# One broadcast of B for two scans: the first product moves to the other PSUM bank pair, the second takes the broadcast's place

## The chip, the cores and the metric

The kernel runs on one core of one Trainium2 chip. A core has five engines that run side by side, each through its own queue in order: TensorE (PE in the profile, with its weight loads as PEld), VectorE (DVE), ScalarE (ACT), GpSimd (POOL) and SyncE (SP), which here issues the DMAs. The metric is the device time of one execution, in microseconds (us).

## The reference

The program is a stack of four layers on x of 32 images, 512 channels, 32 x 32 pixels, each layer x = x + f(groupnorm(x)). Layer 0 scales channels by a small network on DCT statistics, layer 1 is a grouped 3 x 3 convolution, layer 3 a channel attention. Layer 2 is the costly one: a state space model (SSM) over the pixels of each image, on three resolutions (1024, 256 and 64 positions), in both directions. Cut to what matters:

```python
def _ssm(x, xw, dtw, dtb, Al, Dv, g, be):
    xd = jnp.einsum('bdl,kd->blk', x, xw)
    dts, Bs, Cs = xd[..., :R_DT], xd[..., R_DT:R_DT + n], xd[..., R_DT + n:]
    delta = jax.nn.softplus(jnp.einsum('blr,dr->bld', dts, dtw) + dtb)
    A = -jnp.exp(Al)
    dA = jnp.exp(delta[..., None] * A)
    dBx = delta[..., None] * Bs[:, :, None, :] * xt[..., None]
    def step(h, inp):
        da, dbx, c = inp
        h = h * da + dbx
        return (h, jnp.einsum('bdn,bn->bd', h, c))
    _, ys = lax.scan(step, h0, (dA, dBx, Cs))     # over the positions
    return _layernorm(ys + xt * Dv, g, be)
```

There are 256 channels d and 16 states n. B (Bs above) depends on the state and the position alone, not on the channel.

## The kernel before, in words

Every matrix has 128 partitions. For the scans a partition is a pair of a channel and a state: 32 channels times 4 states. One scan instruction of VectorE runs over the 1024 positions of all 128 pairs at once. The 256 channels are 8 groups of 32 and the 16 states are 4 sets of 4, so one direction on the finest resolution has 8 x 4 = 32 scans; the image has two such directions (64 scans), and the two coarser resolutions together take 20 more.

`fine` (L1232) does one direction of the finest resolution. It goes over the two halves d of the channels, in each over the four sets k of states, and in each over the four channel groups q. For each (d, k, q), which is one unit of the schedule, it records these operations:

- TensorE (L1264 to L1266): a broadcast. Two matmuls with a selection matrix, `sel_b[:, k]`, copy the rows of B for the states of set k to the 32 partitions of each state, for 512 positions each. The result fills `pb`, a pair of PSUM banks. It depends on k and not on q.
- ScalarE (L1273): `da` = exp(delta x A), from `dt` in SBUF, where `dt[q]` holds delta x and delta for the channel group q, copied to the states by DMA.
- VectorE (L1279): the product `pb` = `dt` x `pb`, in place in PSUM.
- VectorE (L1212): the scan, from `da` and `pb` into `h` in SBUF.
- GpSimd (L1287): `h` = `h` x `cb`, where `cb` holds C, copied by DMA.
- TensorE (L1295), after each four units: sums over the states into the PSUM banks `y` and `y1b`. After four sets of states VectorE adds the skip term (L1309).

`both` (L1349) does the same for the coarser resolutions, with a broadcast in L1393 or L1400, the product in L1407, `da` in L1435 or L1444, and two scans, one in each direction, from the same product.

The work around the scans belongs to other images and layers: the DCT (L617), the convolution (L899), the dense products of layer 2 (`dense`, L952, called from `scan_inputs`, L989, and from the output), the convolutions that halve the resolution (`down_conv`, L974), `prepare` (L1046), which makes delta, B and C, layer norms (L1142 to L1165) and the last layer (L1670). All run between the scans of the current image.

The order is set by a planner. `Plan.op` records each operation with its engine, an assumed duration, what it reads and writes, and a key, a due time (100 per image, of which a unit of the scans takes 100 / 84). `Plan.order` then plays the recorded operations through: at every moment, each engine takes the ready operation with the smallest key, and the order that results is built as the fixed order of each engine. A `Clock` counts units; `ck.key(a)` is the due time of a units before the current one. The names of line 43 are such leads: `B_AHEAD` for the broadcast, `A_AHEAD` for `da`, `L_AHEAD` for the loads of `dt`, `DB_AHEAD` for the product. The names above it give when other work is due; `INPUTS` is the stretch over which `scan_inputs` makes f1, the input of the scans, and `DOWN` the due time of `down_conv`, which reads f1.

Buffers come from rings. The ring `pb` has two members, each a pair of PSUM banks (L288); `da` has two, `h` six. A ring may be a line (first come, first served by key): then its buffers are given out in the order of their keys, and a buffer's key is that of the first operation that touches it unless it is set by hand. An operation is not taken until the ring has a free member for it and it is that buffer's turn. A member is free once the last operation that uses it has ended.

Of the kernel before, what the change touches and what calls it, by code (L numbers as in the profile page):

```python
# [15 lines left out]
HW = 1024  # L16
# [12 lines left out]
UNITS = 84  # L29

FRONT = (30.9, 63.6)
INPUTS = (109.0, 112.0)
Z = (86.2, 90.1)
DOWN = 114.3
LOWER = (11.8, 36.0)
# [4 lines left out]
SPECTRA = (51.7, 128.4)  # L40
EVACUATE = 85.0
LN_LATE = 10.1
B_AHEAD, A_AHEAD, L_AHEAD, DB_AHEAD = 5.8, 5.9, 14.7, 1.3


class Buf:
# [192 lines left out]
def kernel(ctx: ExitStack, tc: tile.TileContext, t: dict, out: bass.AP):  # L239
    nc = tc.nc  # L240
# [155 lines left out]
    pl = Plan(rings)  # L396
# [16 lines left out]
    def pe(fn, dur, r, w, key, acq=()):  # L413
        return pl.op("PE", dur, fn, r, w, key, acq)
# [757 lines left out]
    def raised(y1, y2, key):  # L1172

        for d in range(2):
            for h in range(2):
                for a in range(2):
                    def go(d=d, h=h, a=a):
                        o = y1.t[:, d, halves[h]].rearrange("p (r a k b) -> p r a k b", a=2, k=16, b=2)
                        i = y2.t[:, d, :].rearrange("p (r k o) -> p r k o", k=16, o=1)
                        nc.gpsimd.tensor_add(  # L1180
                            o[:, :, a], o[:, :, a],
                            i[:, 8 * h : 8 * h + 8].to_broadcast([P, 8, 16, 2]),
                        )

                    pool(go, 256, [(y1, (d, h)), (y2, d)], [(y1, (d, h))], key)
# [46 lines left out]
    def fine(lv, f, pre, S, rev, ck):  # L1232


        sb, cd, dd = pre.pop(f"{lv}_{HW}")
        pl.cross = pl.BESIDE
        if rev:
            raised(S["y1"], S["y2"], ck.key())
        pl.cross = pl.CROSS
        yv = []  # L1240
        for d in range(2):
            acc = [pl.buf("y0"), pl.buf("y1b")]
            dt = []
            for q in range(4):
                ch = slice((d * 4 + q) * 32, (d * 4 + q + 1) * 32)
                z = pl.buf("dt")
                dt.append(z)
                spread(
                    lambda z=z: z.t, lambda i, ch=ch: dd.t[:, ch, :].rearrange("a c l -> c a l"),
                    P * HW * 8, [(dd, (d, h)) for h in range(2)], [z], ck.key(L_AHEAD - q),  # L1250
                )
            for k in range(NS // NQ):
                cb = pl.buf("cb")
                spread(
                    lambda cb=cb: cb.t,
                    lambda i, k=k: cd.t[k * NQ + i : k * NQ + i + 1].to_broadcast([32, HW]),
                    P * HW * 4, [cd], [cb], ck.key(5),
                )
                hs = []
                for q in range(4):  # L1260
                    g = d * 4 + q
                    pb, da, h = pl.buf("pb"), pl.buf("da"), pl.buf("h")

                    def bcast(pb=pb, k=k):  # L1264
                        for cols in halves:
                            nc.tensor.matmul(  # L1266
                                pb.t[:, cols], lhsT=sel_b[:, k, :], rhs=sb.t[:, cols],
                                start=True, stop=True,
                            )

                    pe(bcast, 0.55, [sb], [pb], ck.key(B_AHEAD))
                    act(
                        lambda da=da, z=dt[q], k=k, g=g: nc.scalar.activation(  # L1273
                            da.t, z.t[:, 1, :], AF.Exp, scale=A[lv][:, k, g : g + 1]
                        ),
                        HW, [dt[q]], [da], ck.key(A_AHEAD), True,
                    )
                    dve(
                        lambda pb=pb, z=dt[q]: nc.vector.tensor_mul(pb.t, z.t[:, 0, :], pb.t), HW,  # L1279
                        [dt[q], pb], [pb], ck.key(DB_AHEAD),  # L1280
                    )
                    pl.op(
                        "DVE", 2.21, lambda h=h, da=da, pb=pb: scan(h.t, da.t, pb.t, rev), [da, pb], [h],
                        ck.key(),
                    )
                    pool(
                        lambda h=h, cb=cb: nc.gpsimd.tensor_mul(h.t, h.t, cb.t), HW, [h, cb], [h],  # L1287
                        ck.key(),
                    )
                    hs.append(h)  # L1290
                    ck.u += 1
                for i, cols in enumerate(halves):
                    def add(i=i, cols=cols, hs=hs, acc=acc, k=k):
                        for q in range(4):
                            nc.tensor.matmul(  # L1295
                                acc[i].t[q * 32 : (q + 1) * 32, :], lhsT=sel_y, rhs=hs[q].t[:, cols],
                                start=(k == 0), stop=(k == NS // NQ - 1),
                            )

                    pe(add, 1.3, hs, [acc[i]], ck.key(2))  # L1300
            y = pl.buf("yv")
            yv.append(y)
            dma(
                lambda y=y, d=d: nc.sync.dma_start(y.t, f.t[d]), P * HW * 4, [(f, d)],
                [(y, 0), (y, 1)], ck.key(8),
            )
            for i, cols in enumerate(halves):
                dve(
                    lambda i=i, cols=cols, acc=acc, y=y, d=d: nc.vector.scalar_tensor_tensor(  # L1309
                        y.t[:, cols], in0=y.t[:, cols], scalar=Dv[lv][:, d : d + 1], in1=acc[i].t,  # L1310
                        op0=ALU.mult, op1=ALU.add,
                    ),
                    HB, [(y, i), acc[i]], [(y, i)], ck.key(3),
                )
        pl.cross = pl.BESIDE
        if not rev:
            S["y1"] = pl.buf("y1")
        y1 = S["y1"]
        for i, cols in enumerate(halves):
            yb = [(yv[d], i) for d in range(2)]  # L1320

            def yc(d, cols=cols):
                return yv[d].t[:, cols]

            def yo(d, cols=cols):
                return y1.t[:, d, cols]

            ob = [(y1, (d, i)) for d in range(2)]
            layer_norm(
                lv, yc, yb, yc if rev else yo, yb if rev else ob, HB, ck.key() + (0.0 if rev else LN_LATE)  # L1330
            )
            if not rev:
                continue
            g = pl.buf("g2")
            for d in range(2):
                dma(
                    lambda d=d, g=g, cols=cols: nc.sync.dma_start(g.t[:, d, :], S["zs"].t[d, :, cols]),
                    P * 2048, [(S["zs"], (d, i)), yb[d]], [(g, d)], ck.key(),
                )
                pool(  # L1340
                    lambda d=d, yo=yo, yc=yc: nc.gpsimd.tensor_add(yo(d), yo(d), yc(d)), HB,
                    [yb[d], ob[d]], [ob[d]], ck.key(),
                )
                pool(
                    lambda d=d, yo=yo, g=g: nc.gpsimd.tensor_mul(yo(d), yo(d), g.t[:, d, :]), HB,
                    [ob[d], (g, d)], [ob[d]], ck.key(),
                )

    def both(lv, f, pre, ysum, below, n, ck):  # L1349


        sb, cd, dd = pre.pop(f"{lv}_{n}")
# [21 lines left out]
        for d in range(2):  # L1374
            dt = pl.buf("dt")
# [9 lines left out]
                )  # L1385
            for k0 in range(0, 4, nk):
                pb = pl.buf("pb")

                def bcast(pb=pb, k0=k0):
                    for h in range(2):  # L1390
                        if nk == 1:
                            src = sb.t.rearrange("p (o l) -> p o l", o=1).to_broadcast([96, 2, n])
                            nc.tensor.matmul(  # L1393
                                pb.t[:, halves[h]].rearrange("p (o l) -> p o l", o=2),
                                lhsT=sel_b[:, k0, :], rhs=src, start=True, stop=True,
                            )
                            continue
                        for k in range(h * nk // 2, (h + 1) * nk // 2):
                            src = sb.t.rearrange("p (o l) -> p o l", o=1).to_broadcast([96, 4, n])
                            nc.tensor.matmul(  # L1400
                                pieces(pb.t)[:, k, :, :], lhsT=sel_b[:, k0 + k, :], rhs=src,
                                start=True, stop=True,
                            )
# [21 lines left out]
                for r in range(2):  # L1425
                    da, h = pl.buf("da"), pl.buf("h")
# [302 lines left out]
    def begin(b):  # L1729
# [10 lines left out]
        else:  # L1740
            p0 = 100.0 * (b - 2)
            front(b, st[b], p0 + FRONT[0], p0 + FRONT[1])
            scan_inputs(
                st[b], p0 + INPUTS[0], p0 + INPUTS[1], (p0 + Z[0], p0 + Z[1]), p0 + DOWN
            )
# [134 lines left out]
```

## Time and profile before

| | us |
|---|---|
| median of 3 runs | 11386.0 (11367.82 to 11386.98) |
| profiled execution | 11408.22 |
| its span | 11406.1 |
| TensorE busy | 9375.9 |
| VectorE busy | 9938.1 |
| ScalarE busy | 8259.6 |
| GpSimd busy | 9544.0 |
| of VectorE: 2688 scans | 6069.7 |
| of VectorE: 2048 products of `fine` | 2462.4 |
| of TensorE: 4096 broadcast matmuls of `fine` | 1390.4 |
| of GpSimd: 2048 multiplications with `cb` | 4818.1 |

The span goes from the first instruction to the last; the device time is some 2 us more. "Busy" is time in which the engine works on an instruction. A row of a group names the line, the engine, the operation, what it writes and reads, its shape and count, and after the bar its busy time in us, the mean of one in ns, and the idle time of the engine just ahead of it with what ended most of that. A row of the waits names who waited, for whom, how many us in all, how many times, and the longest. The granted clock is the share of TensorE's full clock that the chip allowed; its mean here is 0.861.

### The profile page before, as it was taken

Reading aid. Unit: us, or ns where it says so; the run is one execution under the profiler, and the core shown is the slowest. Engines: PE = TensorE matmul, PEld = TensorE weight load, DVE = VectorE, ACT = ScalarE, POOL = GpSimd, SP = SyncE. Lnnn points to the kernel's source line nnn. Section 1 sums busy time; section 2 is a strip of 40 time slices with the busy share of each in tenths; the row PEclk is TensorE's granted clock in tenths of the full one; section 3 lists DMA queues with packets and bytes.
Section 4 is the critical chain, followed back from the end, with each engine's and each line's share of the span. In section 5 each row is a group of like instructions: output and inputs, shape, how many; then the busy total and the mean of one; then the engine's idle time right before and its main releaser. Section 6 shows DMA issues by size and latency. Waiting matters only on the chain. (4 is left out here: it accounts for less than half of the span.)

```text
span 11406.1 us, 152013 instructions
## 1 busy us (share of the span) xinstructions
PE 9375.9 (82%) x47512; PEld 4155.3 (36%) x47512; DVE 9938.1 (87%) x8861; ACT 8259.6 (72%) x15684; POOL 9544.0 (84%) x7759
## 2 busy tenths in 40 slices
PE   7888888888888888888888888888888888878765
PEld 4444433334333343333333343333433333332221
DVE  1875889998899989999899999899889998999997
ACT  4677777777778777777777777777777776667664
POOL 2775878898889888888888988898888898889885
PEclk7888889888889888898888988898898987888877
DMA  5665677776767777777767777777677766776654
GB/s 153 167 173 164 182 197 195 186 194 186 212 179 202 188 188 191 204 198 202 191 183 189 204 199 189 189 189 186 190 199 196 187 180 181 199 192 185 168 134 136
DMA packets 931019, 2116.80 MB, mean 186 GB/s; under 512 B 240033, under 2 KB 372537, under 8 KB 917785
## 3 DMA queue, kind: packets, MB, share of 16 engines
q1 hardware_dynamic: 930192, 2107.01, 69.5%
q8 instruction: 376, 6.16, 0.2%
q14 instruction: 433, 3.55, 0.1%
q10 hardware_dynamic: 18, 0.09, 0.0%
HBM read 1677.04 MB, written 429.52 MB: 185 GB/s over the span
## 5 line engine op out<-in xcount | busy, mean ns | idle before, releaser
L1212 DVE TENSOR_TENSOR_SCAN h_all<-da,pb 128x1024 f32<-128x1024 f32 x2688 | 6069.7, 2275 | 296.2 <-ACT da L1435 78.3
L1287 POOL TENSOR_TENSOR h_all<-h_all,cb 128x1024 f32<-128x1024 f32 x2048 | 4818.1, 2363 | 859.9 <-DVE h_all L1212 582.7
L1273 ACT ACTIVATE da<-dt,w_Al 128x1024 f32<-128x1024 f32 x2048 | 2337.1, 1145 | 1171.5 <-DVE h_all L1212 902.5
L1279 DVE TENSOR_TENSOR pb<-dt,pb 128x1024 f32<-128x1024 f32 x2048 | 2462.4, 1218 | 322.7 <-PE pb L1266 276.1
L1266 PE MATMUL pb<-sb,sel_b 96*128 96x512 bf16 x4096 | 1390.4, 426 | 888.0 <-DVE h_all L1212 797.2
L1455 POOL TENSOR_TENSOR h_all<-h_all,cb 128x1024 f32<-128x1024 f32 x640 | 1509.3, 2363 | 20.8 <-DVE h_all L1212 7.4
L1266 PEld LDWEIGHTS <-sel_b 96*128 96x128 bf16 x4096 | 402.4, 107 | 2032.8 <-issue 1998.0
L952 PE MATMUL mm<-x,wt 128*128 128x512 f32 x2048 | 1027.8, 626 | 54.8 <-ACT x L482 18.9
L899 PE MATMUL mm<-pk,wk 99*32 99x512 f32 (+1 forms) x6024 | 904.2, 688 | 113.8 <-DMA pk<-in_xp 19.9
L1444 ACT ACTIVATE da<-dt,w_Al 128x255 f32<-128x255 f32 x2048 | 899.4, 500 | 97.6 <-DVE h_all L1212 79.7
L1295 PE MATMUL y<-h_all,w_sel_y 128*32 128x512 f32 x4096 | 784.4, 724 | 33.5 <-POOL h_all L1287 27.2
L617 PE MATMUL mm<-w_dct,sx 128*128 128x128 f32 x3968 | 651.2, 319 | 94.6 <-ACT sg L460 24.7
L617 PEld LDWEIGHTS mm<-w_dct,sx 128*128 128x128 f32 x3968 | 583.6, 225 | 237.7 <-ACT sg L460 50.1
L1295 PE MATMUL y1b<-h_all,w_sel_y 128*32 128x512 f32 x4096 | 647.7, 663 | 0.0
L952 PE MATMUL mm<-y,w_out_w 128*128 128x512 f32 x1024 | 576.2, 655 | 0.1
L952 PEld LDWEIGHTS mm<-x,wt 128*128 128x128 f32 x2048 | 387.5, 198 | 492.5 <-issue 284.5
L1112 POOL TENSOR_TENSOR g<-g,g 128x512 f32<-128x512 f32 (+2 forms) x384 | 392.9, 1023 | 144.6 <-ACT g L1111 134.5
L1096 PE MATMUL mm<-xd,dtw 64*128 64x512 f32 (+2 forms) x768 | 417.4, 628 | 79.2 <-ACT xd L1066 11.7
L1142 PE MATMUL mm<-ln,ones_d 128*128 128x512 f32 (+1 forms) x768 | 433.1, 662 | 59.9 <-ACT ln L1154 30.7
L1407 DVE TENSOR_TENSOR pb<-dt,pb 128x1024 f32<-128x1024 f32 x320 | 387.7, 1218 | 108.5 <-PE pb L1393 86.6
L974 PE MATMUL mm<-f,wt 128*128 128x256 f32 (+1 forms) x1984 | 421.6, 357 | 21.7 <-ACT f L982 6.0
L1142 PE MATMUL mm<-yv,ones_d 128*128 128x512 f32 x640 | 380.6, 691 | 40.1 <-ACT mm L921 7.2
(292 smaller groups left out, 16188.4 us busy)
## 6 DMA issues: line engine op xcount, KB each, us to landing
dt<-dd SPq DMA_DIRECT2D x2048, 256.0 KB, 7.3
cb<-cd SPq DMA_DIRECT2D x2048, 128.0 KB, 4.8
pk<-in_xp SPq DMA_DIRECT2D x753, 297.0 KB, 5.5
dd<-g SPq DMA_DIRECT2D x256, 512.0 KB, 5.1
xr<-x SPq DMA_DIRECT2D x128, 512.0 KB, 6.3
yv<-fs SPq DMA_DIRECT2D x128, 512.0 KB, 5.1
dt<-ddm SPq DMA_DIRECT2D x512, 128.0 KB, 3.9
sx<-in_x SPq DMA_DIRECT2D x124, 512.0 KB, 4.7
```

What stands on the lines that cost most here:

```text
L617: nc.tensor.matmul(ps.t[:, j * P : (j + 1) * P], lhsT=sx.t[:, 1, i : i + P], rhs=dct, start=True, stop=True,)
L899: nc.tensor.matmul(ps.t[32 * q : 32 * q + 32, r0 * IMG : r1 * IMG].rearrange("p (r k) -> p r k", k=IMG), lhsT=wk.t[:, q, 32 * dy : 32 * dy ...
L952: nc.tensor.matmul(ps.t, lhsT=w(k)[:, m * P : (m + 1) * P], rhs=r()[:, cols], start=(k == 0 and not opened), stop=(k == len(rhs) - 1),)
L1142: lambda d=d: nc.tensor.matmul(ps.t[:, 0:n], lhsT=ones_d, rhs=of(d), start=(d == 0), stop=(d == 1)),
L1212: nc.vector.tensor_tensor_scan(v[0], v[1], v[2], 0.0, ALU.mult, ALU.add)
L1266: nc.tensor.matmul(pb.t[:, cols], lhsT=sel_b[:, k, :], rhs=sb.t[:, cols], start=True, stop=True,)
L1273: lambda da=da, z=dt[q], k=k, g=g: nc.scalar.activation(da.t, z.t[:, 1, :], AF.Exp, scale=A[lv][:, k, g : g + 1]),
L1279: lambda pb=pb, z=dt[q]: nc.vector.tensor_mul(pb.t, z.t[:, 0, :], pb.t), HW,
L1287: lambda h=h, cb=cb: nc.gpsimd.tensor_mul(h.t, h.t, cb.t), HW, [h, cb], [h],
L1295: nc.tensor.matmul(acc[i].t[q * 32 : (q + 1) * 32, :], lhsT=sel_y, rhs=hs[q].t[:, cols], start=(k == 0), stop=(k == NS // NQ - 1),)
L1444: lambda da=da, quads=quads, q=q, g=g, body=body, k0=k0: nc.scalar.activation(pieces(da.t)[:, 0, q, body], quads(1)[:, q, body], AF.Exp, s ...
L1455: lambda h=h, k0=k0: nc.gpsimd.tensor_mul(pieces(h.t), pieces(h.t), cbv()[:, k0 : k0 + nk, :].rearrange("p k (o l) -> p k o l", o=1).to_br ...
```

## The change

In `fine`, two channel groups that follow each other now share one broadcast. For an even q a buffer `src` is broadcast, and a second buffer `pb` is taken from the same ring. The first product reads `src` and writes `pb`; the second product, of the odd q, reads `src` and writes `src`. The first scan reads `pb`, the second `src`. The keys of the two buffers are set by hand, 2.9 and 1.0 units ahead, since an operation that comes late would otherwise set them; the `pb` of the coarser resolutions gets a key of 2.9 units ahead too, in place of its broadcast's. Three constants are changed: the end of `INPUTS`, `B_AHEAD` and `DB_AHEAD`. In the changed kernel the lines of `fine` stand some 8 further down: the broadcast is L1273, the product L1287, the multiplication with `cb` L1295, the sums L1303, the skip term L1317, the product of `both` L1416.

```diff
-INPUTS = (109.0, 112.0)
+INPUTS = (109.0, 123.2)
...
-B_AHEAD, A_AHEAD, L_AHEAD, DB_AHEAD = 5.8, 5.9, 14.7, 1.3
+B_AHEAD, A_AHEAD, L_AHEAD, DB_AHEAD = 8.0, 5.9, 14.7, 1.8
...
-                    pb, da, h = pl.buf("pb"), pl.buf("da"), pl.buf("h")
-
-                    def bcast(pb=pb, k=k):
+                    da, h = pl.buf("da"), pl.buf("h")
+
+
+                    if q % 2 == 0:
+                        src, pb = pl.buf("pb"), pl.buf("pb")
+                        src.key, pb.key = (ck.key(2.9), len(pl.ops)), (ck.key(1.0), len(pl.ops))
+                    else:
+                        pb = src
+
+                    def bcast(pb=src, k=k):
                         for cols in halves:
...
-                    pe(bcast, 0.55, [sb], [pb], ck.key(B_AHEAD))
+                    if q % 2 == 0:
+                        pe(bcast, 0.55, [sb], [src], ck.key(B_AHEAD))
...
-                        lambda pb=pb, z=dt[q]: nc.vector.tensor_mul(pb.t, z.t[:, 0, :], pb.t), HW,
-                        [dt[q], pb], [pb], ck.key(DB_AHEAD),
+                        lambda pb=pb, src=src, z=dt[q]: nc.vector.tensor_mul(pb.t, z.t[:, 0, :], src.t), HW,
+                        [dt[q], src], [pb], ck.key(DB_AHEAD),
...
             for k0 in range(0, 4, nk):
                 pb = pl.buf("pb")
+                pb.key = (ck.key(2.9), len(pl.ops))
```

## The prediction

> **What bounds the kernel now.** First the page's busy shares and its slices: three engines stand close together.
>
> ```profile
> PE 9375.9 (82%) x47512; PEld 4155.3 (36%) x47512; DVE 9938.1 (87%) x8861; ACT 8259.6 (72%) x15684; POOL 9544.0 (84%) x7759
> ```
>
> The windows split that into stages (columns: busy time and count of each engine, then granted clock, DMA share and rate):
>
> ```profile
> 2000.00:4000.00 2000.00, 1686.23 (x8588) 732.10 (x8587) 1823.93 (x1628) 1515.08 (x2886) 1744.00 (x1412) 0.87 0.72 192
> 10000.00:11000.00 1000.00, 779.51 (x3566) 294.49 (x3566) 926.48 (x729) 693.55 (x1226) 890.61 (x679) 0.84 0.66 174
> 11000.00:11406.00 406.00, 238.84 (x727) 70.39 (x725) 328.16 (x279) 195.40 (x282) 255.60 (x159) 0.74 0.52 140
> ```
>
> In the steady part VectorE works 91% of the time, GpSimd 87%, TensorE 84%. VectorE is the fullest, so what ends its idle time sets the pace: 11406.1 - 9938.1 = 1468 us idle, about 230 us of it in the first 285 us, where it has almost nothing to do. Third, who it waits for:
>
> ```profile
> DVE pb L1279 <- PE pb L1266: 276.1, 246, 8.2
> DVE sms L663 <- POOL sms L657: 133.9, 27, 30.6
> DVE pb L1407 <- PE pb L1393: 86.6, 68, 5.1
> DVE h_all L1212 <- ACT da L1435: 78.3, 54, 6.0
> DVE yv L1309 <- PE y L1295: 70.9, 35, 6.4
> ...
> DVE sms L469 <- PE mm L466: 46.8, 23, 6.0
> DVE h_all L1212 <- PE y1b L1295: 45.6, 50, 3.4
> DVE h_all L1212 <- ACT da L1273: 39.8, 47, 4.1
> DVE pb L1279 <- DMA dt<-dd: 39.4, 38, 3.1
> ```
>
> The largest entry is the product (L1279) that waits for the broadcast (L1266), the very pair that the change touches; most of the others are results of TensorE too. Fourth, TensorE's own waits show that the two block each other:
>
> ```profile
> PE pb L1266 <- DVE h_all L1212: 797.2, 703, 5.6
> ```
>
> At 703 of the 2048 broadcasts TensorE stood still, 1.13 us each, because the bank pair to be written was still read by a scan, and everything behind it in its queue stood too. Last, the groups with the durations used below:
>
> ```profile
> L1212 DVE TENSOR_TENSOR_SCAN h_all<-da,pb 128x1024 f32<-128x1024 f32 x2688 | 6069.7, 2275 | 296.2 <-ACT da L1435 78.3
> L1273 ACT ACTIVATE da<-dt,w_Al 128x1024 f32<-128x1024 f32 x2048 | 2337.1, 1145 | 1171.5 <-DVE h_all L1212 902.5
> L1279 DVE TENSOR_TENSOR pb<-dt,pb 128x1024 f32<-128x1024 f32 x2048 | 2462.4, 1218 | 322.7 <-PE pb L1266 276.1
> L1266 PE MATMUL pb<-sb,sel_b 96*128 96x512 bf16 x4096 | 1390.4, 426 | 888.0 <-DVE h_all L1212 797.2
> L1266 PEld LDWEIGHTS <-sel_b 96*128 96x128 bf16 x4096 | 402.4, 107 | 2032.8 <-issue 1998.0
> L1407 DVE TENSOR_TENSOR pb<-dt,pb 128x1024 f32<-128x1024 f32 x320 | 387.7, 1218 | 108.5 <-PE pb L1393 86.6
> ```
>
> **What the Trainium skill says.** "Perfetto Trace Analysis", Identifying the Most-Contended Engine, takes occupancy as a fair measure for Vector and GpSimd but not for TensorE; that is why I rank VectorE first by its 87% and judge TensorE by its stops. The same page, Optimization Strategy, says that repeating gaps can mean that there is not enough SBUF or PSUM for the next tile: the 703 stops of the broadcast, each ended by a scan, agree. "VectorE: DVE Perf Modes", Why PSUM operands drop a tier, holds any fp32 operation with a PSUM operand to the plain rate, so a product that reads one bank pair and writes the other should last as long as one in place; the trace has only the in-place form (1218 ns). "TensorE: Matmul & The Clock Gate", What's actually happening, says that activity releases the throttle; the windows agree (TensorE busy 84%, clock 0.87; 78%, 0.84; 59%, 0.74), and this is a price of taking work away.
>
> **The change part by part.**
>
> *The broadcast.* Half of the 4096 matmuls of L1266 go: 1390.4 / 2 = 695 us of TensorE busy time and 201 us of weight loads. Not all of it is gained. Between the first two windows the clock falls 0.03 for 0.06 less busy share. TensorE's share goes from 0.82 to about 8681 / 11200 = 0.775, so I estimate the clock 0.024 lower, 2.8% longer matmuls, 8681 x 0.028 = 240 us back: 455 us freed. TensorE is not the fullest engine, so this counts only through VectorE's waits.
>
> *The wait of the product.* This is the main term. For every product I laid the trace's VectorE row against the built program's order, which names the bank pair of each product and scan. The cover of a broadcast is what VectorE does between the last scan of that pair and the product that needs it filled again:
>
> ```
> in between            before: products, us waited   after: first products
> nothing                    128,  76.1                      0
> one product                699, 114.7                      0
> one scan                   751,  57.3                    883
> product and scan           435,  29.7                    108
> more                        33,   0                       32
> ```
>
> A broadcast of two matmuls takes 1390.4 / 2048 = 0.68 us busy and longer with its hand-over, so a cover of one product (1.2 us) is too short and one scan (2.3 us) mostly enough. In the changed program the short covers are gone: the first scan of a pair frees the other bank pair, the broadcast runs under the second scan, and the second product of a pair needs no broadcast. At the old rates: 883 x 0.076 + 108 x 0.068 + 32 x 0.076 at most = 77 us instead of 276, that is -200 us. Bounds: -276 (no wait left) and 0 (the longer covers are eaten by TensorE's queue).
>
> *TensorE's other results.* L1407 (86.6) and the entries of L1309 on y and y1b, L469, L459 (two), L1153 and L1212 on y1b (70.9 + 26.2 + 46.8 + 30.1 + 29.2 + 31.7 + 45.6) make 367 us of VectorE waiting on TensorE. It has 455 us less to do, and with half the broadcasts at the old share and length of stops also about 400 us fewer stops. I take a quarter, -92; bounds 0 and a half, -184.
>
> *The moved product.* 1024 products write another bank pair: cost 0; were they 2% slower, 1024 x 0.024 = 25 us. They still take one PSUM input. A first product now needs both pairs, so it can no longer be put between the two scans of the pair ahead. That adds a wait only where the second of these scans is itself late, and behind it stands VectorE's whole row. Scans waited 78 + 40 + 39 = 157 us for da before; 0, with +40 as the bound if a quarter more comes of it.
>
> *Keys.* B_AHEAD 8.0 lets TensorE take the broadcast ahead of more of its other work once its pair is free; what that costs is the blocking case below. DB_AHEAD 1.8 puts both products ahead of the first scan more often; it asks for dt earlier, which cost 39.4 us before: 0, bound +40. INPUTS spreads the four f1 products over 14% of an image instead of 3%. Behind them on TensorE are the down convolutions, and behind those the coarse scans; in the built order VectorE work between the last down convolution and the first coarse product is as long as before (mostly 50 to 120 us in both), so 0, bounds -15 and +30 (L1407 waited 14.6 us for ddc). The new key on the coarse pb only sets its place among the bank pairs: in the order its broadcasts have no more cover than before, 0.
>
> *What is late next.* -200 - 92 = -292 us of VectorE idle time. A product that comes sooner meets da (ACT: 78 + 40 + 39 us in all before), dt by DMA, and GpSimd, 87% full. ACT's own idle time ahead of da is mostly waiting for scans (902 of 1171 us), so it follows VectorE rather than holds it; I give back a third, +97. Sum: -195 us.
>
> The profiled execution took 11408.2 us, 2 us more than its span, so 11213 for that one; the median of the runs shown is 22 us lower, 11386.0 - 195 = 11191. Forecast 11190.
>
> **The rivals.**
>
> *TensorE was the hidden bound.* For it: its busy and stopped time, 9376 + 797 us, rivals VectorE's 9938. Then two thirds of 276 + 86.6 + 280 = 643 us of VectorE's waits on it go, and nothing comes back: -430, 10955. Against it: GpSimd at 87% comes close behind.
>
> *The wait only moves.* The products stop waiting for broadcasts and the scans wait for da, cb's multiplication or dt instead. For it: in the order the leads of ACT, DMA and the remaining TensorE results are the same as before, and GpSimd is nearly as full. Then 0 to -60: 11355. Against it: ACT waits for scans 902 us, so it has room.
>
> *The broadcast blocks TensorE (slower).* Both bank pairs now serve one pair of scans, so each of the 1024 broadcasts is tied to the first scan of the pair ahead, and TensorE, taking it first, stands until that scan ends. If each stands a whole scan, 1024 x 2.3 = 2355 us instead of 797, less the 455 freed: +1103 us of TensorE. Before, 276 us of product waits came with 797 us of stops, 0.35 to one; so +386 - 200 = +186: 11570. It decides from 797 + 455 + 200 / 0.35 = 1823 us of stops, 1.8 us a broadcast. Against it: a broadcast stopped 0.39 us on the mean, and a stop while VectorE is busy harms only what is queued behind.
>
> That the change does not do what it says is excluded: the built program has 2048 matmuls of this kind and 2048 products.
>
> **How the numbers follow.** Forecast 0.50 (its own range 11090 to 11300), hidden bound 0.18, moved wait 0.14, blocking 0.18. A change under 0.2% (23 us) can't be told from none here. Faster by more: 0.50 + 0.18 + 0.07 = 0.75, less 0.01 for the forecast's tail = 0.74; same 0.05 (from the moved wait); slower 0.18 + 0.03 = 0.21. The range reaches from 10930, just past the hidden bound, to 11420, the moved wait with the keys' +40; most of the blocking case is left out.
>
> **What would show it.** Right: the wait of the first product (L1287 then) for its broadcast under 120 us; VectorE 88 to 90% busy with unchanged busy time; TensorE busy near 8900 with a clock near 0.84; its stops at the broadcast near 400 us. Wrong: those stops above 1800 us, waits of scans for da or of L1309 for y grown by more than 200 us together, or a product clearly above 1218 ns.

## The result, and the profile after

The changed kernel takes 11295.67 us (median of 4 runs, 11285.95 to 11315.67); the kernel before, run beside it, takes 11384.6 us. The ratio is 0.9924, with a 95% interval of 0.9912 to 0.9936: faster by 0.76%, or 89 us, where 195 us were forecast. The profiled execution took 11294.69 us, 113.5 us less than that of before; the latter lay some 22 us above its median.

The busy shares on the page of the changed kernel:

```profile
PE 9004.9 (80%) x45464; PEld 3951.5 (35%) x45464; DVE 9955.1 (88%) x8861; ACT 8260.1 (73%) x15684; POOL 9544.7 (85%) x7759
```

TensorE lost 371 us of busy time. Who VectorE waits for (who, for whom, us in all, times, longest):

```profile
DVE sms L663 <- POOL sms L657: 146.4, 28, 29.4
DVE pb L1287 <- PE pb L1273: 116.0, 104, 5.9
DVE pb L1287 <- DMA dt<-dd: 89.9, 69, 5.1
DVE h_all L1212 <- ACT da L1444: 68.3, 61, 4.7
DVE h_all L1212 <- ACT da L1281: 64.8, 51, 4.4
DVE pb L1416 <- PE pb L1402: 59.5, 47, 5.6
...
DVE yv L1317 <- PE y L1303: 44.4, 24, 8.0
```

The product's wait for its broadcast fell from 276 to 116 us, and its wait for `dt` rose from 39 to 90. TensorE's own stops:

```profile
PE pb L1273 <- DVE h_all L1212: 563.1, 351, 11.1
PE y L1303 <- POOL h_all L1295: 156.2, 135, 3.8
```

Half as many stops at broadcasts, each longer (1.6 us for 1.13); with less to do, TensorE now also arrives early at the sums and waits there for GpSimd. The groups that answer to those of before, with the sums of the kernel before as the last line:

```profile
L1287 DVE TENSOR_TENSOR pb<-dt,pb 128x1024 f32<-128x1024 f32 x2048 | 2461.5, 1226 | 263.8 <-PE pb L1273 116.0
L1273 PE MATMUL pb<-sb,sel_b 96*128 96x512 bf16 x2048 | 704.7, 430 | 626.9 <-DVE h_all L1212 563.1
L1303 PE MATMUL y<-h_all,w_sel_y 128*32 128x512 f32 x4096 | 949.1, 739 | 159.8 <-POOL h_all L1295 156.2
L1295 PE MATMUL y<-h_all,w_sel_y 128*32 128x512 f32 x4096 | 784.4, 724 | 33.5 <-POOL h_all L1287 27.2
```

The broadcasts' busy time is halved, but that of the sums into `y` rose by 165 us, and that of the sums into `y1b` by 49 (647.7 to 696.7), so part of the saved busy time came back elsewhere on TensorE. One of these matmuls lasts hardly longer (739 ns for 724). Busy time counts what overlaps once, so they overlap less, where TensorE now waits for GpSimd ahead of them.

Laid out by what ended it, VectorE's idle time in the two traces (us; gaps up to 150 ns, which the view of waits leaves out, are a row of their own):

```
                                      before   after
product of fine for its broadcast       276     116
product of both for its broadcast        93      69
other results of TensorE                339     299
ScalarE                                 397     376
GpSimd                                  178     201
DMA                                     102     169
gaps up to 150 ns                        58      82
no wait shown, and the rest              15      15
```

That is 130 us less idle time; against it stand 17 us more busy time (9955.1 for 9938.1), together the 113 us of the span. Two rows grew that no step of the forecast reckoned with: the gaps too short for the view of waits, and the busy time itself. The timeline shows where they come from. A product behind a scan, in the kernel before (start, duration, engine, line):

```profile
4587.99 2.27 DVE L1212 TENSOR_TENSOR_SCAN h_all<-da,pb 128x1024 f32<-128x1024 f32 x1
4590.18 1.21 DVE L1279 TENSOR_TENSOR pb<-dt,pb 128x1024 f32<-128x1024 f32 x1
```

and a first product behind a scan in the changed one (x2: the row goes on over the second product, which follows at once):

```profile
7013.17 2.23 DVE L1212 TENSOR_TENSOR_SCAN h_all<-da,pb 128x1024 f32<-128x1024 f32 x1
7015.51 2.36 DVE L1287 TENSOR_TENSOR pb<-dt,pb 128x1024 f32<-128x1024 f32 x2
```

Before, 4587.99 + 2.27 = 4590.26: the product starts 80 ns before the scan's recorded end. After, 7013.17 + 2.23 = 7015.40: it starts 110 ns behind it. Over the whole trace the median was -82 ns for 733 such products before and +104 ns for the 600 first products that stand right behind a scan now: 186 ns apart. 503 of the products behind a scan have a gap of 85 to 125 ns in the changed kernel, 3 had one before. The built program tells why: the first product overwrites the bank pair which the scan just ahead of it read, so it has to wait for that scan on VectorE's own count; a product in place overwrites its own broadcast and need not wait for the scan ahead.

### The profile page after: what moved, and what is told of

Read it like the earlier page. It is cut to its first block, busy times and chain, and to the rows that moved or that the text cites. A ratio compares the mean times of both kernels' runs of the same rounds, so it can differ in the third digit from the quotient of the medians.

```text
span 11292.9 us, 148195 instructions
## 1 busy us (share of the span) xinstructions
PE 9004.9 (80%) x45464; PEld 3951.5 (35%) x45464; DVE 9955.1 (88%) x8861; ACT 8260.1 (73%) x15684; POOL 9544.7 (85%) x7759
## 5 line engine op out<-in xcount | busy, mean ns | idle before, releaser
L1295 POOL TENSOR_TENSOR h_all<-h_all,cb 128x1024 f32<-128x1024 f32 x2048 | 4817.5, 2363 | 792.0 <-DVE h_all L1212 500.2
L1287 DVE TENSOR_TENSOR pb<-dt,pb 128x1024 f32<-128x1024 f32 x2048 | 2461.5, 1226 | 263.8 <-PE pb L1273 116.0
L1273 PE MATMUL pb<-sb,sel_b 96*128 96x512 bf16 x2048 | 704.7, 430 | 626.9 <-DVE h_all L1212 563.1
L1303 PE MATMUL y<-h_all,w_sel_y 128*32 128x512 f32 x4096 | 949.1, 739 | 159.8 <-POOL h_all L1295 156.2
L1303 PE MATMUL y1b<-h_all,w_sel_y 128*32 128x512 f32 x4096 | 696.7, 664 | 0.0
L1273 PEld LDWEIGHTS <-sel_b 96*128 96x128 bf16 x2048 | 194.9, 105 | 1270.9 <-issue 1257.9
L1112 POOL TENSOR_TENSOR g<-g,g 128x512 f32<-128x512 f32 (+2 forms) x384 | 393.3, 1024 | 163.0 <-ACT g L1111 152.8
L1416 DVE TENSOR_TENSOR pb<-dt,pb 128x1024 f32<-128x1024 f32 x320 | 388.0, 1216 | 92.9 <-PE pb L1402 59.5
```

What stands on the lines that cost most here:

```text
L1273: nc.tensor.matmul(pb.t[:, cols], lhsT=sel_b[:, k, :], rhs=sb.t[:, cols], start=True, stop=True,)
L1287: lambda pb=pb, src=src, z=dt[q]: nc.vector.tensor_mul(pb.t, z.t[:, 0, :], src.t), HW,
L1303: nc.tensor.matmul(acc[i].t[q * 32 : (q + 1) * 32, :], lhsT=sel_y, rhs=hs[q].t[:, cols], start=(k == 0), stop=(k == NS // NQ - 1),)
```

## The experiments

**Is it TensorE's load or the cover?** Each broadcast twice, all else in its place:

```diff
-                        for cols in halves:
+                        for cols in (*halves, *halves):
```

> The changed kernel with each broadcast matmul issued twice into the same banks: every engine's order is that of the changed kernel, TensorE carries 4096 broadcast matmuls again. Theory A (the gain comes from the longer cover, TensorE's lighter load is worth little): 11,300 to 11,340, the product's wait for its broadcast rises from 116 to at most 180 us. Rival B (the gain comes from TensorE's 695 us): the gain goes, 11,370 to 11,420.

Measured: 11386.21 us, ratio to the kernel before 0.9999 (0.9989 to 1.0009). The whole gain is gone. In the view of VectorE's waits of this run:

```profile
DVE pb L1287 <- PE pb L1273: 169.4, 128, 6.3
DVE sms L663 <- POOL sms L657: 150.8, 26, 32.7
DVE pb L1287 <- DMA dt<-dd: 82.6, 66, 4.7
```

The product's wait is within what theory A allowed, 107 us below the kernel before, but the time is not, so theory A falls. Rival B's time was met, but this run does not show that its reason holds. A doubled broadcast also lasts longer itself, and the product has to wait for the whole of it. The same broadcast and product, first in the changed kernel, then in this run:

```profile
744.08 0.60 PE L1273 MATMUL pb<-sb,sel_b 96*128 96x512 bf16 x2
744.72 1.23 DVE L1287 TENSOR_TENSOR pb<-dt,pb 128x1024 f32<-128x1024 f32 x1 [1.26 <-PE pb L1273]
756.35 1.04 PE L1273 MATMUL pb<-sb,sel_b 96*128 96x512 bf16 x4
757.42 1.23 DVE L1287 TENSOR_TENSOR pb<-dt,pb 128x1024 f32<-128x1024 f32 x1 [1.69 <-PE pb L1273]
```

Over all products that wait, the median time from the start of the broadcast to the start of the product is 0.64 us in the changed kernel and 1.08 us here. With 128 such waits that is up to 55 us, and the product's wait grew by 53 (116 to 169). The broadcasts that are waited for start no later behind the last scan of their bank pair than in the changed kernel (median 2.03 us for 2.35). The spans differ by 90 us (11383.0 for 11292.9). So more than half of what was lost is the length of the doubled broadcast, which no kernel with single broadcasts pays, and I estimate what TensorE's lighter load is worth to all else at the other 37 us; 28 of them are VectorE's waits for other results of TensorE. A run that puts the extra matmuls where no product waits for them would settle it; there is none.

**Is it the sharing or the keys?** The three constants alone, on the kernel before:

> The kernel before with the three constants of the change. Theory A (the sharing brings the gain): within 30 us of 11,385. Rival C (the gain is the new keys' alone): near 11,300.

Measured: 11366.7 us, ratio 0.9979 (0.9970 to 0.9988). And the sharing with the old constants:

> The sharing with the three constants of the kernel before. Theory A: 11,280 to 11,320, and the product's wait for dt by DMA falls back from 90 towards 40 us, since DB_AHEAD is 1.3 again. Rival C (keys needed): 11,385 or above.

Measured: 11385.81 us, ratio 0.9990 (0.9979 to 1.0001). Neither half brings the gain alone: theory A is met by the first run and fails in the second, rival C the other way round, so both single-cause theories fall. In the second run the product waits only 104 us for its broadcast, but VectorE waits 383 us for other results of TensorE (299 in the changed kernel) and 428 us for ScalarE (376). The wait for `dt` was to fall towards 40 us there; it was 73, and 49 with the keys alone.

**How far do orders scatter?** A constant that has nothing to do with the change, on both kernels:

```diff
-Z = (86.2, 90.1)
+Z = (85.0, 90.1)
```

> The kernel before with the start of Z at 85.0 in place of 86.2, which has nothing to do with the broadcasts but makes the planner build another order. Theory D (another order alone moves the time little): within 25 us of 11,385. Rival (orders scatter by as much as the change): off by 60 us or more, either way.

Measured: 11380.51 us, ratio 0.9995 (0.9989 to 1.0002).

> The changed kernel with the start of Z at 85.0 in place of 86.2, another order as in the same run of the kernel before, which moved that by -0.05%. Theory D (orders scatter little): within 25 us of 11,296. Rival (they scatter by as much as the keys seem to bring): off by 50 us or more.

Measured: 11273.12 us, ratio to the kernel before 0.9901 (0.9886 to 0.9916), so 0.23% below the changed kernel. Both runs are within theory D's 25 us. Still, another order alone can move the time by a quarter of a per cent; smaller differences between two keys say nothing.

**Which key?** One at a time, DB_AHEAD first:

> The changed kernel with DB_AHEAD back at 1.3. If the extra 50 us of waits for dt come from products that are due earlier: these waits fall from 90 to 40 or 50 us and the time by 20 to 50 us. Rival (the key is what makes the sharing pay): 40 us or more slower, since without its three keys the sharing gave nothing.

Measured: 11269.88 us, ratio to before 0.9893 (0.9875 to 0.9912), faster than the change as it was made. The stated reason doesn't hold, though. Two lines of VectorE's waits in this run:

```profile
DVE pb L1287 <- DMA dt<-dd: 92.6, 72, 6.2
DVE pb L1287 <- PE pb L1273: 81.7, 87, 5.9
```

The wait for `dt` did not fall; what fell is the wait for the broadcast. With the other two keys, both with DB_AHEAD 1.3:

> The sharing with only INPUTS new (123.2), B_AHEAD 5.8 and DB_AHEAD 1.3 as before. With both old it was 11,386, with both new 11,270. Theory F (INPUTS makes the difference: the f1 products no longer come in one lump between other work of TensorE): 11,270 to 11,300. Rival (B_AHEAD does): 11,360 to 11,390.

Measured: 11356.15 us, ratio 0.9968 (0.9956 to 0.9980).

> The sharing with only B_AHEAD new (8.0), INPUTS 112.0 and DB_AHEAD 1.3 as before. Theory F: 11,360 to 11,390. Rival (B_AHEAD makes the difference): 11,270 to 11,300.

Measured: 11313.11 us, ratio 0.9935 (0.9922 to 0.9948). B_AHEAD is worth 0.55% to the sharing (0.9990 to 0.9935), more than the scatter; INPUTS 0.22% alone and 0.42% on top of B_AHEAD (0.9935 to 0.9893), at its edge and above. The first of the two times lies just under its rival's range and the second outside both of its ranges, but theory F named the wrong key as the larger one.

> The sharing with DB_AHEAD 1.3, INPUTS 123.2 and B_AHEAD 10.0. If taking the broadcast ever earlier is what helps: 11,230 to 11,265. If 8.0 already puts it ahead of all that matters: within 20 us of the 11,270 that B_AHEAD 8.0 gave.

Measured: 11275.04 us, ratio 0.9906 (0.9891 to 0.9921): within the 20 us of the second expectation, so 10.0 brings no more than 8.0.

> The sharing with B_AHEAD 8.0, INPUTS 123.2, DB_AHEAD 1.3 and the start of Z at 85.0. Each of the last two alone took some 25 us off the changed kernel. If they add up: 11,245 to 11,260. If they are two draws of the same scatter: 11,260 to 11,300.

Measured: 11260.06 us, ratio 0.9893 (0.9879 to 0.9906): on the border of the two expectations. The ratio is the same as without the second constant, so it does not show that they add up. These two, at 0.9893, are the best of the kernels run, 0.3% below the changed one.

**What are the 104 ns?** First try, with an idle multiplication in the gap. `moved` marks the first products, `last` is the operation issued on VectorE just before; 2.21 is the planner's duration of a scan:

```diff
         for o in order:
             for b in o.acq:
                 b.t = tiles[b.ring][b.slot]
+            if o.eng == "DVE":
+                if getattr(o, "moved", False) and last and last.dur == 2.21:
+                    nc.vector.tensor_mul(pad, ones_d[:, 0:PAD], ones_d[:, 0:PAD])
+                last = o
             o.fn()
```

> The changed kernel with an idle VectorE multiplication of 128x100 (a result that nobody reads) put straight ahead of each first product that stands right behind a scan, 600 in all; every other instruction keeps its place. In the changed kernel such a product starts 104 ns after the scan's end, where an instruction that doesn't touch what the scan read starts 82 ns ahead of it, so 600 times 186 ns = 112 us. Theory E (this is a wait of the product for the scan whose bank pair it overwrites): the extra work of some 0.15 us fits into it, so the time stays within 20 us of the changed kernel's 11,296, and the product starts within some 30 ns of the end of the extra instruction. Rival (the product starts late for another reason, such as reading a pair that was just broadcast): 600 times 0.15 us are added, 11,370 to 11,400.

Measured: 11623.06 us, ratio 1.0206 (1.0184 to 1.0227). Neither expectation fits: 327 us more. The extra instruction isn't what I took it for (its line's durations as minimum, median and maximum in ns):

```profile
L1801 DVE TENSOR_TENSOR pad<-ones_d x600: 225/520/9224, 262.6 to 11541.7; 128x100 f32<-128x100 f32 x150
```

The shortest took 225 ns and the longest 9.2 us, 551 us in all. Both its inputs lie in SBUF. The Trainium skill, "GPSIMD Engine Reference", Specifications, says that GpSimd's SBUF interfaces are shared with VectorE and contended for by VectorE instructions with two SBUF inputs; this trace agrees. Of the 550 that began while GpSimd worked on an elementwise operation of two tensors, 545 ended only after it had ended, 120 ns after on the median. The test was repeated with an instruction of one input, `nc.vector.bn_stats(pad, ones_d[:, 0:PAD])`:

> As the run with a multiplication ahead of 600 first products, but the extra instruction takes statistics over 128x100 elements of one SBUF tensor: one tensor input, where that multiplication took two inputs from SBUF and lasted 0.2 to 9.2 us. Theory E (the product waits for the scan right ahead of it, whose bank pair it overwrites): the extra work of 0.15 us runs in that gap, within 25 us of the changed kernel's 11,296. Rival (the gap belongs to the product itself and would follow the extra instruction too): 600 times 0.15 us are added, 11,370 to 11,400.

Measured: 11311.7 us, ratio to before 0.9929 (0.9915 to 0.9943), where the changed kernel has 0.9924. The 600 instructions cost nothing that can be told from none. Of the 553 that began while such an operation of GpSimd ran, 515 ended before it did. VectorE's timeline in that run:

```profile
7023.78 2.27 DVE L1214 TENSOR_TENSOR_SCAN h_all<-da,pb 128x1024 f32<-128x1024 f32 x1
7025.97 0.23 DVE L1801 BATCH_NORM_STATS2 pad<-ones_d 128x6 f32<-128x100 f32 x1
7026.15 1.23 DVE L1289 TENSOR_TENSOR pb<-dt,pb 128x1024 f32<-128x1024 f32 x1
```

The instruction in the middle starts 80 ns ahead of the scan's end, and the product stays where it was: from the scan's end to the product's start the median of the 600 is 104 ns, with an instruction of 240 ns in between as without it. So it waits for the scan to be done with, as theory E has it; that is shown.

**What does such time cost at the end?** The same kind of instruction, of 128 columns, ahead of 600 products behind a scan in the kernel before, where the gap isn't there to hide it:

> The kernel before with an idle VectorE instruction (statistics over 128x128 elements of one SBUF tensor, some 0.19 us from the end of the scan ahead to its own end) ahead of the first 600 products that stand right behind a scan; there the product waits for nothing on VectorE, so the work is added: 600 times 0.186 us = 112 us of VectorE time, as much as the gaps of the changed kernel. Theory G (such time reaches the end nearly whole, and is what the forecast lacked): 11,465 to 11,500. Rival (it hides behind the idle time that VectorE has anyway): 11,385 to 11,420.

Measured: 11446.47 us, ratio 1.0059 (1.0047 to 1.0072), by the ratio 67 us more. VectorE's busy time grew by 109 us:

```profile
PE 9362.9 (82%) x47512; PEld 4148.8 (36%) x47512; DVE 10047.5 (88%) x9461; ACT 8264.9 (72%) x15684; POOL 9544.1 (83%) x7759
```

So of 1 us more on VectorE about 0.6 us reach the end, between the two expectations.

**Can the gap be avoided?** With the first product in SBUF. `db` is a new ring of two bf16 buffers of 1024 columns, so this product is rounded to bf16; for room in SBUF there are five `h` buffers, and a run with only that beside it.

```diff
-H_TILES = 6
+H_TILES = 5
...
+        "db": ([P, HW], BF16, 2, True),
...
-                        src, pb = pl.buf("pb"), pl.buf("pb")
-                        src.key, pb.key = (ck.key(2.9), len(pl.ops)), (ck.key(1.0), len(pl.ops))
+                        src, pb = pl.buf("pb"), pl.buf("db")
+                        src.key = (ck.key(2.9), len(pl.ops))
```

> The changed kernel with five h buffers in place of six; only to compare the next run with. 11,300 to 11,400.

Measured: 11777.92 us, ratio 1.0341 (1.0320 to 1.0362), far above the expectation. The largest of VectorE's waits is now that of a scan for the sums, which free an `h` buffer (26 us in the changed kernel):

```profile
DVE h_all L1212 <- PE y1b L1303: 479.9, 223, 6.2
```

> Sharing with the first product written to SBUF, into two buffers of bf16 (so this product is rounded to bf16; SBUF has no room for fp32), with five h buffers. The broadcast now needs one bank pair for two scans and the other is free to be filled two scans ahead, and no first product overwrites what the scan right ahead of it read in the usual order. Theory E and the cover: against the run with five h buffers the gaps of 104 ns go (-60 to -110 us) and so does most of the product's wait for its broadcast (-80 to -110 us); 120 to 200 us faster than that run. Rival (neither costs anything on the path): within 30 us of it.

Measured: 12748.75 us, ratio 1.1193 (1.1169 to 1.1217), 8% slower than the run with five `h` buffers, against both expectations. VectorE's groups in that run, the two kinds of scan first:

```profile
L1213 DVE TENSOR_TENSOR_SCAN h_all<-da,pb 128x1024 f32<-128x1024 f32 x1664 | 3779.9, 2277 | 798.4 <-PE y1b L1304 501.7 <-issue 54.7 <-POOL da L1440 42.0
L1213 DVE TENSOR_TENSOR_SCAN h_all<-da,db 128x1024 f32<-128x1024 f32 x1024 | 3184.4, 3110 | 13.5 <-ACT da L1282 12.1 <-POOL h_all L1296 0.4
...
L1288 DVE TENSOR_TENSOR db<-dt,pb 128x1024 bf16<-128x1024 f32 x1024 | 1224.6, 1198 | 46.8 <-PE pb L1274 42.9
```

A scan of `da` and `db`, both in SBUF, takes 3110 ns on the mean and not 2277, and GpSimd's multiplications with `cb` last 2661 ns for 2360 in the run with five `h` buffers. In PSUM the product keeps off that. The gaps did go: of the first products behind a scan 1 has a gap of 85 to 125 ns, and 498 of 531 start ahead of the scan's end, where the run with five `h` buffers has 511 products with such a gap. But what this was worth can't be read from a run that lost so much elsewhere. The product's wait for its broadcast, which was to fall by 80 to 110 us, is 43 us for 40: with five `h` buffers there was little of it left to save.

## Why the prediction was half right

The direction was right, the size was not: in the profiled executions -113 us for -195. Three terms of the sum fell short by about 40 us each: the rate at which a cover still waits, the share of TensorE's other results, and the moved product, which was put at nothing. By its own steps:

- *The wait of the product*, -200 us forecast: -160. No short cover was left, as the order said, but the rate taken from before did not hold. 883 covers of one scan were priced at 0.076 us each and cost 116 us, 0.131 each. In 103 of 104 cases that still wait, it was such a cover. Where the first product still waits, TensorE most often hadn't stopped for anything near it: it was busy with other work, the sums (L1303) most of all. That a cover of one scan waits as long as it did before was the wrong assumption; how long depends on what else stands in TensorE's row.
- *TensorE's other results*, -92 forecast: the same entries went from 367 to 313 us, -54. TensorE's busy time fell to 9005, not near 8900, and its stops at broadcasts to 563, not 400. The clock that was to take 240 us back hardly fell: 0.859 for 0.861, where 0.84 was forecast; what came back was 214 us in the sums. The busy share alone doesn't tell the clock: the doubled run has 0.871 at 82%, the kernel before 0.861 at 82%.
- *The moved product, cost 0, at most 25 us*: this is the step whose reason failed, not only its size. It asked only whether the product itself lasts longer (1229 ns for 1206 behind a scan) and not what it must wait for on its own engine: 503 gaps of about 104 ns in place of an overlap of 82 ns are an estimated 94 us. Part of it came back by something else that was not foreseen: in the built order 156 scans stand right behind their own product, 378 before, and in the trace of before such a scan starts 103 to 133 ns behind it, some 0.2 us later than without the wait, so 222 fewer are about 44 us back. In sum the short gaps and the busy time grew by 24 + 17 = 41 us. At the 0.6 us per us of the kernel before, the 94 us alone would be an estimated 57 us of the time.
- *The keys, cost 0*: wrong. With the old ones the sharing gives 0.9990. B_AHEAD, whose cost the forecast moved into the blocking case, is worth 0.55% to it. INPUTS was priced by the way from the down convolutions to the coarse scans, which did not change (L1416 waits 15.4 us for ddc, L1407 14.6 before), and still brought something, at the edge of the scatter when alone. The wait for `dt` grew by 50 us, near the bound of 40 given to DB_AHEAD, but stayed when DB_AHEAD went back, so that wasn't its cause. It came mostly with the sharing: 73 us with the old keys, 49 with the keys alone.
- *What is late next*, +97 forecast: DMA +67, GpSimd +23, ScalarE -21, and -10 of TensorE's results outside the entries above: with the rest some +60. It was too high, and it was `dt` and not `da` that came late. That this error ran against the others is luck: without it the forecast would have missed by more.

Together, the cover fell short by 40 us, the other TensorE waits by 38, the moved product cost 41 net, and the give-back was some 37 smaller: 82 us, the gap between -195 and -113. The blocking rival did not come: stops of 563 us, far from 1823. The hidden bound did not come either: its 430 us stand against 113 in all, and against an estimated 37 for the load by the doubled broadcasts.

What stays open: how much of the gain is TensorE's lighter load and how much the longer cover, since doubling the broadcasts makes them longer too; what makes `dt` late; the keys of the bank pairs that are set by hand, which no run varied; and why the sharing with the old keys waits more for TensorE's other results and ScalarE. The waits say that they come later in the order, not which of the moved operations does it. With a scatter of 0.23% between orders, the 0.3% that DB_AHEAD 1.3 brings is at the edge of what can be put down to the key.

## What to carry to other kernels

Where an instruction is given a new place for its result, ask what last read that place and on which engine: if it is the instruction right ahead on its own engine, the overlap with it is lost, in gaps too short for a list of waits. Doing a cheap broadcast once less need not be worth its busy time (686 us less of it gave 89 us here), and the gain may need the schedule to be set anew before it shows. An experiment that puts work back to test an engine's load should not also lengthen what others wait for. Before a difference of some tenths of a per cent is read as an effect of a key, one unrelated change of order tells how far orders scatter.

## What the runs showed of the hardware

- A wait on VectorE's own last instruction costs 186 ns here: a product starts 104 ns after the scan's recorded end where it overwrites what the scan read, and 82 ns ahead of it where it doesn't wait. The Trainium skill, "VectorE: DVE Perf Modes", The DRAIN you can't avoid, has it that the semaphore costs nothing extra in a measured chain of copies; here, behind a scan, the wait costs time, and the measurement decides.
- A VectorE instruction with two inputs from SBUF, beside a GpSimd that is 82% busy, took 225 to 9224 ns for 128x100 elements, and 545 of the 550 that began during an elementwise operation of GpSimd ended only after it; one with a single SBUF input took 226 to 267. A scan with both inputs in SBUF took 3110 ns on the mean, with one in PSUM 2277.
- One `h` buffer of six is worth 4.2% of the time (ratios 1.0341 and 0.9924), far more than the change itself.
